# Gate products beside the row sums, transposes in TensorE's gaps, and vector work moved away from a norm and a search

## The chip, the cores and the metric

The kernel runs on one core of a Trainium2 chip. A core has five engines that work side by side, each through a queue of its own in order: TensorE (PE; its weight loads are listed as PEld), VectorE (DVE), ScalarE (ACT), GpSimd (POOL) and SyncE (SP, which issues most of the DMA transfers). They wait for each other by semaphores. The metric is the device time in microseconds (us); the time of a kernel is the median of its runs.

## The reference

Two transformer layers over 32 sequences ("batches") of 128 tokens, width 512, in float32. What matters here is the first layer, in which every step but the last is needed in full before the next can be closed:

```python
h = _ln(x, ln1_g, ln1_b) + shift
qkv = (h @ Wqkv.T).reshape(b, n, 3, H, HD)              # 16 heads of 64
q = _ln(q, qn_g, qn_b); k = _ln(k, kn_g, kn_b)          # per head
attn = softmax(q @ k.T / sqrt(HD)); o = attn @ v
x = x + o @ Wout.T
gate = softmax(tok @ Wgate.T)                            # 4096 tokens, 8 experts
vals, idx = top_k(gate.T, 512)                           # each expert takes 512 tokens
g = _ln(tok[idx], mlp_g, mlp_b)
y = gelu(g @ fc1s.T + b1s) @ fc2s.T + b2s                # per expert, hidden width 2048
tok = tok.at[idx].add(y * vals)
```

The second layer is attention (16 heads of 32) and an MLP, both with a scale and a shift that come from the condition vector ("adaLN").

## The kernel before

**Planner.** The kernel is not written in the order in which it runs. Each operation is registered with `sch.op(engine, us, fn, w=..., r=..., prio=..., job=...)`: its engine, an assumed duration, what it writes and reads, a priority (lower goes first) and a job. `Sched.run` then simulates the engines with these durations and emits for each engine, at every step, the operation that can start first, ties broken by the priority. A few jobs are open at once. Tiles come from four pools: 52 rows (`row`, 128 x 512 float32), small tiles (`sml`), the 8 PSUM banks (`bank`) and 11 weight slots. An operation whose tile has no free slot is not taken. `also=` names another engine that may do the operation: `tt` (L1130 on, its instructions at L1137 for VectorE and L1138 for GpSimd) uses it for elementwise sums, `copy` for copies by ScalarE or VectorE (L1128, L1129). Each engine executes its list in that fixed order.

**Start.** The projection of the condition (`ada`, L1197, into `pa`), the transposes of the first normed tokens (`tpx`), a small sum (`pu_a`), then the first qkv products (`pq`, L1316).

**Attention.** `pair(g)` takes two batches. All large products are done by a scheme of seven products of half size in place of eight, with sums of operands ahead (`os`, `tv`, `hsa`) and of results behind (`comb`, `onto`, `out2`). For each batch: the head norms by a Newton iteration on VectorE (`newton`, L299 to L307, whose result is `rs`), the scaling of q and k by it (L1463), transposes (`tpq`), scores (`sc`, L1495), exponentials (`pe`), row sums (`sums`, L1511, into `ps`) and the weighted values (`outs`, L1517). `back` does this for one batch, and the batch's gates.

**Gates.** The gate of a batch is linear in x and in the attention output, so it is computed from the transposed input (`xT`, loaded by `gate_T`) and `oT` without waiting for the projection: `gates` (L1553) puts twelve products of 32 columns into four strips of TensorE (`pgz`), the copy `zg` brings them to SBUF, and `add_up` (L1562) sums the strips by a product with a selection matrix (`pg`). A row-sum product uses TensorE in the same four strips. In a pair, the first batch's gates run in one operation with the second batch's row sums (`gates_sums`); the second batch's gates run by themselves. After each pair a softmax on VectorE and ScalarE writes `g_all` and a DMA adds the gates to the tokens' rows in `tok`.

**Late projections.** For the last 16 batches `oT` is stored (`otd`), and `late_projection` (through `project`, products `w` at L1595, additions to `xl`) runs during the choice of tokens.

**Choice of tokens** (from L1674). A search over 30 bits for each expert's 512th largest gate: count on VectorE (`junk`, L1691), sum over partitions on TensorE (`pc`, L1693), two updates on VectorE (`drop` L1695, `cand` L1697). Then prefix sums, and for each expert `expert_tokens(e)`: four one-hot tiles on VectorE (`oh`, L1762), values (`val`), 32 small products on TensorE (`pi`, L1782), and the indices `idx`.

**Experts.** `expert(e)` gathers its tokens by indirect DMA from GpSimd's queue (`xg`, L1826, which needs all stores to `tok`), norms them (`ng`), transposes them (`tpg`), and multiplies by `fc1` (`u`, L1935) and `fc2` (`d`, L1999). The sums of the `fc1` blocks (`s`, `fc`) are made by GpSimd, four for each of four blocks.

**Second layer.** At its beginning: `adaln` products (`pad`), the bias `pb0` (L2208), the norm of the first tokens and their transposes (`a_0t`), then the products `qk` (L2301).

Of the kernel before, what the change touches and what calls it, by code (L numbers as in the profile page):

```python
# [19 lines left out]
P = 128  # L20
# [225 lines left out]
def mm_us(n, count=1):  # L246

    return count * 2 * max(2 * n / 2400 + 0.0025, 0.11)
# [17 lines left out]
class Stage:  # L266
# [12 lines left out]
    def row(self, name, shape=(P, D)):  # L279
        return Buf(self.rows, list(shape), F32, name)  # L280

    def sml(self, name, n):
        return Buf(self.smls, [P, n], F32, name)
# [745 lines left out]
def fast_kernel(ctx: ExitStack, tc: tile.TileContext, x, condT, mask, cols, w_ada, wqkv, wout, wout_p, wout_o, wgate,  # L1029
# [17 lines left out]
    def const_tile(name, shape, dtype=F32):  # L1047
        return const.tile(list(shape), dtype, name=name)
# [6 lines left out]
    make_identity(nc, ident)  # L1055
    ones_f = const_tile("ones_f", (P, 64))
# [58 lines left out]
    def bcast(a, n):  # L1115

        return a.unsqueeze(2).to_broadcast([a.shape[0], a.shape[1], n])
# [32 lines left out]

    scratch, scratch2 = row("scratch", (P, D)), row("scratch2", (P, D))
# [136 lines left out]
    def pair(g):  # L1288
# [6 lines left out]
        lg, oT = sml(f"lg_{g}", 2 * E), []  # L1295
# [95 lines left out]
        for i in range(2):  # L1391
            sch.op(DVE, 0.19, lambda i=i: nc.vector.tensor_scalar(var[i].t, var[i].t, 1.0 / HD0, EPS, ALU.mult, ALU.add),
                   w=[var[i]], r=[var[i]], prio=pp + 10 + 100 * i, job=job)
            rs = st.newton(var[i], 2 * H0, f"qk_{b0 + i}", pp + 10 + 100 * i, job)
            if i == 0:
                zs, ahead = row(f"zg_{g}", (P, 2, S)), None
            oT_, ahead = back(b0 + i, i, job, lg, qk[i], v[i], rs, zs, ahead)
            oT.append(oT_)
        if b0 >= NB - LATE:
            late_projection(g)  # L1400
        else:
            project(g, oT, [x_b[b0], x_b[b0 + 1]], b0 * 100 + 142, job)

        pg = b0 * 100 + 150
        gm, gs = sml(f"gm_{g}", 2), sml(f"gs_{g}", 2)
        lv = lambda a: a.rearrange("p (n e) -> p n e", e=E)
        sch.op(DVE, 0.17, lambda: nc.vector.tensor_reduce(gm.t, lv(lg.t), AX.X, ALU.max), w=[gm], r=[lg], prio=pg, job=job)
        sch.op(DVE, 0.17, lambda: nc.vector.tensor_tensor(lv(lg.t), lv(lg.t), bcast(gm.t, E), ALU.subtract),
               w=[lg], r=[lg, gm], prio=pg, job=job)
        sch.op(ACT, 0.25, lambda: nc.scalar.activation(lg.t, lg.t, AF.Exp), w=[lg], r=[lg], prio=pg, job=job, table="exp")  # L1410
        sch.op(DVE, 0.17, lambda: nc.vector.tensor_reduce(gs.t, lv(lg.t), AX.X, ALU.add), w=[gs], r=[lg], prio=pg, job=job)
        sch.op(DVE, 0.17, lambda: nc.vector.reciprocal(gs.t, gs.t), w=[gs], r=[gs], prio=pg, job=job)
        sch.op(DVE, 0.17, lambda: nc.vector.tensor_tensor(
            g_all[:, b0 : b0 + 2, :], lv(lg.t), bcast(gs.t, E), ALU.mult), w=[(g_b, g)], r=[lg, gs], prio=pg, job=job)
        sch.op(SP, 0.06, lambda: nc.sync.dma_start(
            tok[b0 * S : (b0 + 2) * S, D:].rearrange("(b p) e -> p b e", p=P), g_all[:, b0 : b0 + 2, :]),
            w=[(tok_b, -1 - g)], r=[(g_b, g)], lat=3.0, prio=pg, job=job)

    statd = dram.tile([NB // 2, 4, S], F32, name="statd")
# [33 lines left out]
    def back(b, i, job, lg, qk, v, rs, zs, ahead):  # L1453
# [3 lines left out]
        late = b >= NB - LATE  # L1457
        qkT = [row(f"qkT_{b}_{j}", (P, 4, S)) for j in range(4)]
# [60 lines left out]
        if i == 0:  # L1519
            sch.op(PE, mm_us(D), sums, w=[ps], r=pe[0] + pe[1], prio=pa + 3, job=job)  # L1520
        else:

            def gates_sums(gates0=ahead[0]):
                gates0()
                sums()
            sch.op(PE, mm_us(S, 3) + mm_us(D), gates_sums, w=[ps, ahead[1]], r=pe[0] + pe[1] + ahead[2], prio=pa + 3, job=job)
            copy([(zs, 0)], [ahead[1]], lambda: zs.t[:, 0, :], lambda p_=ahead[1]: p_.t, S, pa + 3, job)
# [7 lines left out]
        def gate_T(pr):  # L1535

            t_ = row(f"xT_{b}", (P, DC, S))
            sch.op(SP, 0.06, lambda: nc.sync.dma_start(t_.t, xT[b]), w=[t_], r=[qkT[0]], lat=3.0, prio=pr, job=job)
            return t_
# [15 lines left out]
        if i:  # L1555
            pg = bank(f"pg_{b}", (P, 2, E))
            sch.op(PE, mm_us(S, len(parts) // DC), gates, w=[pz], r=need, prio=pgt, job=job)
            copy([(zs, 1)], [pz], lambda: zs.t[:, 1, :], lambda: pz.t, S, pgt, job)

            def add_up():  # L1560
                for n in range(2):
                    nc.tensor.matmul(pg.t[:, n, :], zs.t[:, n, :], sel[:, :E], start=True, stop=True)  # L1562
            sch.op(PE, mm_us(E, 2), add_up, w=[pg], r=[zs, cst_b], prio=pgt, job=job)
            sch.op(DVE, 0.16, lambda: nc.vector.tensor_copy(lg.t, flat(pg)), w=[lg], r=[pg], prio=pgt, job=job)
# [4 lines left out]
        return oT, (gates, pz, need)  # L1569
# [13 lines left out]
    def project(g, oT, xt, pr, job):  # L1583
        A = lambda i, j: oT[i - 1][j - 1]
        S_ = {i: row(f"os{i}_{g}", (P, 4, S)) for i in (1, 2, 3, 4)}
        for i, a_, b_, op_ in ((1, A(2, 1), A(2, 2), ALU.add), (2, S_[1], A(1, 1), ALU.subtract),
                               (3, A(1, 1), A(2, 1), ALU.subtract), (4, A(1, 2), S_[2], ALU.subtract)):
            tt(lambda i=i: S_[i].t, lambda a_=a_: a_.t, lambda b_=b_: b_.t, op_, D, [S_[i]], [a_, b_], pr - 1, job)
# [17 lines left out]
        def onto(a_, i, l):  # L1606

            tt(lambda: half(i, l), lambda: half(i, l), lambda: a_.t, ALU.add, HD, [(xt[i - 1], l)], [(xt[i - 1], l), a_], pr + 1, job)
# [45 lines left out]
    def late_projection(g):  # L1654
        pr = RP + 700 + 2 * g
        oT = [[row(f"ol_{2 * g + i}_{n}", (P, 4, S)) for n in range(2)] for i in range(2)]
        xt = [row(f"xl_{2 * g + i}") for i in range(2)]
        loads = [(oT[i][n], otd[2 * g + i - NB + LATE, n], [(otd_b, (2 * g + i, n))]) for i in (1, 0) for n in range(2)]
        for b_, src, r_ in loads + [(xt[i], x[2 * g + i], []) for i in range(2)]:
            sch.op(SP, 0.06, lambda b_=b_, src=src: nc.sync.dma_start(b_.t, src), w=[b_], r=r_, lat=3.0, prio=pr - 60, job=RJ, spare=20)  # L1660
        project(g, oT, xt, pr, RJ)
# [92 lines left out]

    def expert_tokens(e, pr, job, after=()):
# [28 lines left out]
        sch.op(PE, 1.0, gather, w=[pi], r=[*oh, val], prio=pr, job=job)  # L1784
        pv = lambda: pi.t.rearrange("p (h two) -> p h two", two=2)
# [25 lines left out]
    def expert(e, after):  # L1811
# [25 lines left out]
        for m in range(NM):  # L1837
# [11 lines left out]
            tt(lambda A=A, Sq=Sq: Sq(1), lambda A=A: A(2, 1), lambda A=A: A(2, 2), ALU.add, D, [(g, 1)], [(f, 1)], pw_, job, POOL, False)  # L1849
# [64 lines left out]
        if e == 0:  # L1914
            sums0.append(Tg[4])
            saw(PR + 5, job, [Tg[4]])
            expert_tokens(1, RP + 750, job)
# [287 lines left out]
    for i in (1, 2):  # L2205
        def bias0(i=i):
# [5 lines left out]
           prio=LB - 700, job=LJ)  # L2212

# [475 lines left out]
```

## Time and profile before

| | |
|---|---|
| median of 3 runs | 3215.75 us (3213.43 to 3215.94) |
| profiled execution, its time | 3212.72 us |
| its span, first to last instruction | 3211.0 us |
| TensorE busy | 3170.7 us |
| VectorE busy | 2262.4 us |
| ScalarE, GpSimd busy | 959.4, 713.1 us |
| mean granted TensorE clock | 0.996 |

The profile is one execution, recorded by the hardware profiler. Busy is the time in which an engine executes; the ends of matmuls are modelled, so that they overlap their successors by a little, and what counts is the distance from start to start. A line of the timeline gives start, duration, engine, source line, operation, `out<-in`, shapes, and `xN` for N merged instructions; in brackets stands the idle time before it. A wait names the engine that waited, what it was about to do, and what released it. PEclk is the share of TensorE's full clock that the chip granted. A float32 product shows as two matmul instructions.

By stages the execution goes: start to 14 us; attention to 965; late projections and choice of tokens to 1067; experts to 1877; second layer to the end.

### The profile page before, as it was taken

What the parts mean: (1) busy time and instruction counts of PE and PEld (TensorE: products, weight loads), DVE (VectorE), ACT (ScalarE), POOL (GpSimd) and SP (SyncE); (2) the same over time, 40 slices, a digit from 0 to 9 for tenths busy, and PEclk for the clock granted to TensorE, in tenths of its full rate; (3) what the DMA queues carried; (4) which work ended last, traced back from release to release, by engine and by line L of the source; (5) the groups of instructions that cost most, each with busy time, mean ns of one, the idle gap of its engine ahead of it and who ended that gap; (6) DMA issues with size and microseconds to landing.
All of it is one profiled execution on the core that took longest, in us unless ns stands there. A gap on an engine that the chain in (4) does not pass through costs nothing.

```text
span 3211.0 us, 55822 instructions
## 1 busy us (share of the span) xinstructions
PE 3170.7 (99%) x21688; PEld 2551.0 (79%) x21688; DVE 2262.4 (70%) x4895; ACT 959.4 (30%) x2299; POOL 713.1 (22%) x559
## 2 busy tenths in 40 slices
PE   8999999999999899999999999999999999999999
PEld 4655665555557788888888889999999999999998
DVE  8877777888867886766666447666666666666665
ACT  3333423444340222221122223333333333333332
POOL 0111111000034348776666500000000000000000
PEclk9999999999999899999999999999999999999999
DMA  4232223222235433344333553333333333333343
GB/s 175 73 103 70 73 71 115 100 99 70 66 121 186 141 92 115 102 112 119 96 110 88 167 184 112 96 98 100 101 101 103 106 105 101 100 101 100 99 138 107
DMA packets 253283, 346.44 MB, mean 108 GB/s; under 512 B 22810, under 2 KB 157522, under 8 KB 252498
## 3 DMA queue, kind: packets, MB, share of 16 engines
q1 hardware_dynamic: 244354, 325.16, 30.5%
q0 software_dynamic: 7168, 16.91, 2.8%
q8 instruction: 174, 2.85, 0.4%
q14 instruction: 99, 0.81, 0.1%
q10 hardware_dynamic: 1488, 0.71, 0.1%
HBM read 288.02 MB, written 54.69 MB: 107 GB/s over the span
## 4 chain that ended last, share of the span: by engine, by line
PE 96%; DVE 2%; DMA 1%; issue 0%; ACT 0%; POOL 0%; SPq 0%; ACTq 0%; DVEq 0%; POOLq 0%
PE m L2481 12%; PE n L2542 12%; PE u L1935 12%; PE d L1999 12%; PE q L1357 11%; PE qk L2301 6%; PE w L1595 6%; PE v L1357 5%; PE v L2347 3%; PE o L2347 3%; PE sc L1495 2%; PE po L1517 2%; PE tpq L1113 2%; PE pq L1316 1%; PE sc L2397 1%; PE ps L1511 1%
## 5 line engine op out<-in xcount | busy, mean ns | idle before, releaser
L2428 POOL TENSOR_TENSOR hi_t<-hi_t,inv 128x512 f32<-128x512 f32 x32 | 40.7, 1272 | 1218.6 <-DVE inv L1148 1218.6
L2492 ACT ACTIVATE m<-m,prm 128x128 f32<-128x128 f32 x512 | 161.8, 389 | 236.6 <-DVE m L2486 232.1
L1999 PE MATMUL d<-fc,h 128*128 128x256 f32 x992 | 219.0, 380 | 0.0
L1999 PEld LDWEIGHTS d<-fc,h 128*128 128x128 f32 x992 | 188.4, 190 | 24.9
L1946 ACT ACTIVATE h<-h,prm 128x256 f32<-128x256 f32 x256 | 115.0, 500 | 256.8 <-DVE h L1940 256.8
L1935 PE MATMUL u<-gT,fc 128*128 128x256 f32 x768 | 179.6, 384 | 0.7 <-ACT gT L1902 0.7
L1935 PEld LDWEIGHTS u<-gT,fc 128*128 128x128 f32 x768 | 148.1, 193 | 21.5 <-ACT gT L1902 1.1
L2486 DVE TENSOR_TENSOR m<-mu,m 128x512 f32<-128x512 f32 x128 | 87.9, 688 | 104.4 <-PE m L2481 101.8
L1323 ACT ACTIVATE sq<-qk 128x512 f32<-128x512 f32 x128 | 81.4, 636 | 220.4 <-DVE qk L1361 212.0
L2486 DVE TENSOR_TENSOR mu<-mu,m 128x512 f32<-128x512 f32 x96 | 65.9, 686 | 85.3 <-PE m L2481 85.1
L2481 PE MATMUL m<-n2a,w_s 128*128 128x128 f32 x1024 | 125.0, 276 | 0.0
L1940 DVE TENSOR_TENSOR h<-v,u 128x512 f32<-128x512 f32 x128 | 86.6, 683 | 50.8 <-PE u L1935 49.1
L2542 PE MATMUL n<-w_t,ms 128*128 128x256 f32 x512 | 122.3, 383 | 0.0
L1935 PE MATMUL u<-tg,s 128*128 128x256 f32 x512 | 121.1, 380 | 0.8 <-DVE tg L1137 0.8
L2481 PE MATMUL m<-n2T,w 128*128 128x128 f32 x1024 | 119.9, 276 | 0.0
L2481 PEld LDWEIGHTS m<-n2a,w_s 128*128 128x128 f32 x1024 | 119.6, 192 | 0.1
L2481 PEld LDWEIGHTS m<-n2T,w 128*128 128x128 f32 x1024 | 118.2, 192 | 1.2 <-DVE n2T L2236 0.2
L2542 PE MATMUL n<-w_t,m 128*128 128x256 f32 x512 | 116.3, 380 | 0.0
L2542 PE MATMUL n<-w,m 128*128 128x256 f32 x512 | 114.7, 383 | 0.0
L1357 PE MATMUL q<-wqkv,hT 128*128 128x512 f32 x240 | 114.5, 605 | 0.0
L1999 PE MATMUL d<-t,hs 128*128 128x256 f32 x512 | 113.5, 380 | 0.0
L1357 PE MATMUL q<-wqkv,hsb 128*128 128x512 f32 x240 | 113.4, 595 | 0.0
(1225 smaller groups left out, 7486.5 us busy)
## 6 DMA issues: line engine op xcount, KB each, us to landing
w_t<-t2d SPq DMA_DIRECT2D x256, 256.0 KB, 3.1
w<-in_w_dram SPq DMA_DIRECT2D x192, 256.0 KB, 4.4
fc<-in_fc_dram SPq DMA_DIRECT2D x64, 512.0 KB, 4.5
fc<-in_fc_dram SPq DMA_DIRECT2D x32, 1024.0 KB, 5.3
x<-in_x_dram SPq DMA_DIRECT2D x32, 256.0 KB, 3.0
xT<-in_xT_dram SPq DMA_DIRECT2D x32, 256.0 KB, 2.7
otd<-oT SPq DMA_DIRECT2D x32, 256.0 KB, 2.1
ol<-otd SPq DMA_DIRECT2D x32, 256.0 KB, 4.3
```

The lines of the kernel that those rows point to most:

```text
L1357: nc.tensor.matmul(ps[m].t, lhs()[:, k, :], rhs[0](k), start=(k == 0), stop=(k == 1))
L1595: nc.tensor.matmul(ps[n].t, lhs.t[:, k, :], rhs(k), start=(k == 0), stop=(k == 3))
L1935: nc.tensor.matmul(ps[n].t[:, t, :], lhs()[:, k, t * P : (t + 1) * P], rhs.t[:, k, :], start=(k == 0), stop=(k == 1))
L1940: sch.op(DVE, dve_us(D), lambda: nc.vector.tensor_tensor(o_.t, a_.t, ps[n].t, ALU.add), w=[o_], r=[a_, ps[n]], prio=pr, job=job)
L1946: sch.op(ACT, act_us(HQ, 1), lambda t=t, c=c: nc.scalar.activation(o_.t[:, t, :], o_.t[:, t, :], AF.Gelu_apprx_tanh, bias=col("b1s", e * 1 ...
L1999: nc.tensor.matmul(ps[n].t[:, j, :], lhs[m].t[:, k, t * P : (t + 1) * P], rhs.t[:, 2 * m + k, :], start=(m == 0 and k == 0), stop=(m == NM ...
L2301: nc.tensor.matmul(ps[m].t[:, z, u, :], w_()[:, k, u * P : (u + 1) * P], rhs()[:, k, :], start=(k == 0), stop=(k == 1))
L2347: nc.tensor.matmul(ps[m].t, lhs()[:, k, :], w_()[:, k, :], start=(k == 0), stop=(k == 1))
L2481: nc.tensor.matmul(ps[n].t[:, u, :], l1w[what].t[:, k, (NQ * q + u) * P : (NQ * q + u + 1) * P], rhs()[:, k, :], start=(k == 0), stop=(k = ...
L2486: sch.op(DVE, dve_us(D), lambda: nc.vector.tensor_tensor(o_.t, a_.t, ps[n].t, ALU.add), w=[o_, *more], r=[a_, ps[n]], prio=pq_, job=job)
L2492: sch.op(ACT, act_us(S, 1), lambda u=u, c=c: nc.scalar.activation(o_.t[:, u, :], o_.t[:, u, :], AF.Gelu, bias=col("b1", c), scale=1.0), w= ...
L2542: nc.tensor.matmul(ps[n].t, Ah[lhs][c // NQ].t[:, c % NQ, :], b_.t[:, k, :], start=(c == 0), stop=(c == 7))
```

## The change

- **Gates.** Every batch's gate products but the last batch's now run with the next batch's row sums, over the border of the pair too (`gq["ahead"]`). `close` copies the strips of four batches into one tile and, at the fourth, sums them (`pg`, read by the softmax straight from PSUM), does one softmax for four batches and one store. The load of `xT` is issued after the second half of `oT` instead of after `qkT`, but for the last batch.
- **Transposes.** `spin(n, dst)` transposes the identity matrix n times into a bank that nobody reads: 44 at the very start, 62 after the last late projection (`ends["xt"]`), 28 after the small products of expert 1's indices (`pis[1]`), 22 after the bias product `pb0` of the second layer.
- **GpSimd.** The first of the four sums of each `fc1` block of expert 0 now also waits for the head norm of the last batch (`ends["rs"]`). In the late projections the sums and additions may no longer go to GpSimd (`also=False`).
- **One-hots.** Those of expert 1 now wait for the last late projection.

```diff
+    def spin(n, dst):
+        for _ in range(n):
+            nc.tensor.transpose(dst[:, :P], ident, ident)
...
+    spun = bank("spun")
+    sch.op(PE, 6.5, lambda: spin(44, spun.t), w=[spun], prio=-2000, job=0)
...
-            if i == 0:
-                zs, ahead = row(f"zg_{g}", (P, 2, S)), None
-            oT_, ahead = back(b0 + i, i, job, lg, qk[i], v[i], rs, zs, ahead)
-            oT.append(oT_)
+            oT.append(back(b0 + i, i, job, qk[i], v[i], rs))
...
+    def close(b, pz, pr, job):
+
+        if b % 4 == 0:
+            gq["zs"] = row(f"zg_{b}", (P, 4, S))
+        zs, n = gq["zs"], b % 4
+        copy([(zs, n)], [pz], lambda: zs.t[:, n, :], lambda: pz.t, S, pr, job)
+        if n < 3:
+            return
+        q, b0 = b // 4, b - 3
+        pg, lg, gm, gs = bank(f"pg_{q}", (P, 4, E)), sml(f"lg_{q}", 4 * E), sml(f"gm_{q}", 4), sml(f"gs_{q}", 4)
+
+        def add_up():
+            for k in range(4):
+                nc.tensor.matmul(pg.t[:, k, :], zs.t[:, k, :], sel[:, :E], start=True, stop=True)
+        sch.op(PE, mm_us(E, 4), add_up, w=[pg], r=[zs, cst_b], prio=pr + 2, job=job)
...
+        sch.op(DVE, 0.19, lambda: nc.vector.tensor_reduce(gm.t, pg.t, AX.X, ALU.max), w=[gm], r=[pg], prio=pr, job=job)
...
+        if b == NB - 1:
+            ends["rs"] = rs
...
-        if i == 0:
+        if b == 0:
             sch.op(PE, mm_us(D), sums, w=[ps], r=pe[0] + pe[1], prio=pa + 3, job=job)
         else:
 
-            def gates_sums(gates0=ahead[0]):
+            gates0, pz0, need0 = gq["ahead"]
+
+            def gates_sums():
                 gates0()
                 sums()
...
+            sch.op(PE, mm_us(S, 3) + mm_us(D), gates_sums, w=[ps, pz0], r=pe[0] + pe[1] + need0, prio=pa + 3, job=job)
+            close(b - 1, pz0, pa + 3, job)
...
-            sch.op(SP, 0.06, lambda: nc.sync.dma_start(t_.t, xT[b]), w=[t_], r=[qkT[0]], lat=3.0, prio=pr, job=job)
+            sch.op(SP, 0.06, lambda: nc.sync.dma_start(t_.t, xT[b]), w=[t_], r=[qkT[0] if b == NB - 1 else oT[1]], lat=3.0,
+                   prio=pr, job=job)
...
-        if i:
-            pg = bank(f"pg_{b}", (P, 2, E))
+        gq["ahead"] = (gates, pz, need)
+        if b == NB - 1:
             sch.op(PE, mm_us(S, len(parts) // DC), gates, w=[pz], r=need, prio=pgt, job=job)
...
+            close(b, pz, pgt, job)
...
+        ends["xt"] = xt
...
-        project(g, oT, xt, pr, RJ)
+
+        project(g, oT, xt, pr, RJ, also=False)
...
-            tt(lambda A=A, Sq=Sq: Sq(1), lambda A=A: A(2, 1), lambda A=A: A(2, 2), ALU.add, D, [(g, 1)], [(f, 1)], pw_, job, POOL, False)
+            tt(lambda A=A, Sq=Sq: Sq(1), lambda A=A: A(2, 1), lambda A=A: A(2, 2), ALU.add, D, [(g, 1)], [(f, 1), *([] if e else [ends["rs"]])], pw_, job, POOL, False)
...
-            expert_tokens(1, RP + 750, job)
+
+            expert_tokens(1, RP + 750, job, ends["xt"])
+            spun0, spun2 = bank("spun0"), bank("spun2")
+            sch.op(PE, 6.7, lambda: spin(62, spun0.t), w=[spun0], r=ends["xt"], prio=RP + 740, job=job)
+            sch.op(PE, 3.0, lambda: spin(28, spun2.t), w=[spun2], r=[pis[1]], prio=RP + 990, job=job)
...
+    spun1 = bank("spun1")
+    sch.op(PE, 2.4, lambda: spin(22, spun1.t), w=[spun1], r=[pb0], prio=LB - 820.5, job=LJ)
```

## The prediction

> **What bounds it now.** I read the page first: busy times, clock row, chain of waits.
>
> ```profile
> span 3211.0 us, 55822 instructions
> ...
> PE 3170.7 (99%) x21688; PEld 2551.0 (79%) x21688; DVE 2262.4 (70%) x4895; ACT 959.4 (30%) x2299; POOL 713.1 (22%) x559
> ...
> PEclk9999999999999899999999999999999999999999
> ...
> PE 96%; DVE 2%; DMA 1%; issue 0%; ACT 0%; POOL 0%; SPq 0%; ACTq 0%; DVEq 0%; POOLq 0%
> ```
>
> TensorE sets the end. Time is saved only by fewer TensorE cycles, less TensorE idling, or a clock that doesn't drop. Second, the waits of TensorE (total, times, longest): they are the whole list of its idling worth more than 1.5 us.
>
> ```profile
> PE tpg L1113 <- DVE xng L1890: 10.2, 1, 10.2
> PE pa L1197 <- DMA wada<-in_w_ada_dram: 8.4, 1, 8.4
> PE tpq L1113 <- DVE qk L1463: 3.1, 1, 3.1
> PE a_0t L1113 <- DVE a_1v L339: 2.8, 1, 2.8
> PE pc L1693 <- DVE junk L1691: 2.1, 4, 0.8
> PE sc L1495 <- DVE qkT L1475: 1.8, 2, 1.6
> ```
>
> Third, the clock. The trace grants half clock in 66.6-70.0, 1070.1-1087.2 and 1889.3-1896.1 us and, by the spacing of the matmuls, before 12.0. I asked for busy times by stretch on the clock's own grid (length, then PE, PEld, DVE, ACT, POOL, clock):
>
> ```profile
> 8.57:11.98 3.41, 3.41 (x16) 1.75 (x15) 1.56 (x6) 0.59 (x1) 0.00 (x0) 1.00 1.05 399
> 937.00:940.40 3.40, 1.58 (x10) 1.32 (x11) 3.37 (x6) 0.78 (x1) 3.22 (x3) 1.00 0.19 69
> 1080.35:1083.77 3.42, 2.76 (x7) 2.20 (x8) 2.53 (x9) 2.01 (x6) 0.85 (x1) 0.50 0.92 323
> 1885.90:1889.31 3.41, 1.09 (x6) 0.61 (x4) 2.35 (x9) 1.07 (x4) 0.00 (x0) 1.00 1.05 407
> ```
>
> A full stretch (first) is followed by full clock; one 81% busy (third) isn't. One with 1.09 us of matmuls (last) is followed by half clock, while the second, 1.58 us busy of which about 1.0 are transposes, keeps full clock. So transposes seem to count as activity. Fourth, the timeline around two gate products (start, duration):
>
> ```profile
> 700.35 0.43 PE L1553 MATMUL pgz<-xT,wg 128*32 128x128 f32 x8
> 700.59 0.62 PE L1553 MATMUL pgz<-oT,ww 128*32 128x128 f32 x16
> 701.02 1.04 PE L1511 MATMUL ps<-pe,ones_f 128*32 128x512 f32 x8
> 701.88 1.93 PE L1517 MATMUL po<-pe,v 128*32 128x128 f32 x64
> ...
> 705.57 1.88 PE L1357 MATMUL q<-wqkv,hsb 128*128 128x512 f32 x4
> 707.38 0.43 PE L1553 MATMUL pgz<-xT,wg 128*32 128x128 f32 x8
> 707.62 0.62 PE L1553 MATMUL pgz<-oT,ww 128*32 128x128 f32 x16
> 708.17 1.98 PE L1357 MATMUL q<-wqkv,hT 128*128 128x512 f32 x4
> ```
>
> And VectorE beside a GpSimd sum and without one:
>
> ```profile
> 931.33 1.26 POOL L1138 TENSOR_TENSOR s<-fc 128x512 f32<-128x512 f32 x1
> 931.44 1.20 DVE L303 SCALAR_TENSOR_TENSOR qk_31t<-qk_31y 128x32 f32<-128x32 f32 x1
> ...
> 935.04 0.19 DVE L303 SCALAR_TENSOR_TENSOR qk_30t<-qk_30y 128x32 f32<-128x32 f32 x1
> ```
>
> **What the Trainium skill says.** "TensorE: Matmul & The Clock Gate", Part 1: the clock is half after an idle window of about 3.4 us and full after a busy one, the window running freely; the grid above agrees. Its Part 4 says full clock doesn't engage for transposes; the second stretch speaks against that, but no run here has transposes alone. "TensorEngine Tiling (Array Packing)", Key Properties: changing the tiling mode drains TensorE; the trace agrees, about 0.1 us each way (below). "SBUF — State Buffer", SBUF: two separate sides: a VectorE instruction with two SBUF inputs and a GpSimd one that reads SBUF exclude each other for a whole instruction; the 1.20 against 0.19 us agrees.
>
> **The change, step by step**, against the profiled execution (3212.72 us; span 3211.0 and 1.7 around it). The median of the runs, 3215.75, lies 3.0 above it; I carry the difference over to the median.
>
> *Gates beside row sums.* A gate product alone: the four q products ahead take 1.81 (705.57 to 707.38) where 4 x 0.43 = 1.72 is their rate, so 0.1 goes to the switch; then 0.79 to the next product. Beside row sums it takes 0.67 (700.35 to 701.02), the switch is already paid by the sums, and these take 0.86 instead of 0.88 where they follow a q product. Saved: 0.10 + 0.12 + 0.02 = 0.24, in the 15 pairs that have a successor: 3.6. The adding up (0.36 and 0.1 of switch per pair, 16 times: 7.4) becomes 8 times 0.72 + 0.1: 6.6, saves 0.8. Together **-4.4** (ends -3 and -5). The small VectorE and ScalarE instructions and the stores of the gates halve, the copy of the sums goes; VectorE is 70 to 84% busy in that stage under a TensorE without idling, so this counts nothing. The load of xT waits for oT instead of qkT: behind it on SP's queue stand the loads of the next pair; it takes 2.7 us to land and is needed only at the next batch's row sums (13 or some 40 us later), so nothing. Without that cover it would be a wait of 2.7 per batch. Three rows of the pool (xT, two oT) are held some 40 us longer in each pair: the profile shows no rows; nothing if there is slack, bounded above under the rivals.
>
> *44 transposes at the start.* Transposes start 0.213 us apart at half clock, 0.107 at full. From 1.6 us (the identity is ready at 1.53), 3.4 to 6.8 us at half clock and the rest at full: end at 8.0 to 9.7, against the weight's landing at 8.43. Then pa takes 1.04 (the row of ps, same shape) instead of 1.94, and eight transposes 1.04 instead of 1.89; the first q product, at 13.83 now, comes 0.5 to 1.3 earlier: **-1.0**. If they stay at half clock, they end at 11.0: +2.6.
>
> *GpSimd's first-expert sums wait for the last norms.* Now three of batch 31's Newton steps take 1.20 to 1.30 instead of 0.19 beside them, ahead of batch 30's on VectorE's queue: these start at 934.8, though their squares are there at 929.7, and TensorE waits 3.1 and then 1.6 us. With the sums behind both norms I give all but a rest back: **-4.2** (0 to -4.7). The 16 sums of 1.27 then run from about 935 to 956; their products stand at 1081, so they have 120 us.
>
> *Late projections on VectorE alone.* In 979-1041 VectorE is busy 50.4 of 62 us; 15 of the 30 updates of the candidate take 0.77 instead of 0.16 beside GpSimd: 9 us go. GpSimd's 24 instructions there come over: 12 x 0.69 + 12 x 0.42 = 13.3. So 54 of 62, and the 2.1 us of waits at pc partly go: **-1.0** (-2 to +8, see the rivals).
>
> *One-hots of expert 1 into the gap, 62 and 28 transposes.* The four one-hots (1.22 each) now delay VectorE's last additions at 1060-1067; without them and GpSimd's additions the last store starts some 0.3 earlier, and so do the gathers. VectorE then does the one-hots from 1067.5 to 1072.5, before the first gathered row lands (1074.6). TensorE: 62 x 0.107 = 6.6 from 1067.5, the product of the indices 0.9, 28 x 0.107 = 3.0: to 1078.0, against 1077.9 for the first transposes. At full clock these end 0.5 earlier, the sixteen products at 1081.01 take 3.5 instead of 6.75; the next transposes then wait for VectorE's xng, which follows the evictions, some 0.5: **-3.9**. Bounds: -4.6 without that wait; +6.4 if the transposes run at half clock after one window: 32 x 0.107 + 30 x 0.213 = 9.8, 0.9, 28 x 0.213 = 6.0, end at 1084.3.
>
> *22 transposes at 1887.* 2.4 us in a gap of 2.8, no delay. Products at half clock in 1889.3-1896.1 cost up to 3.4, but the one at 1897.6 needs VectorE's sums n1a, ready at 1895.5: **-2.0** (-3.4 to +1).
>
> Sum: -4.4 - 1.0 - 4.2 - 1.0 - 3.9 - 2.0 = -16.5: 3196.2 for the profiled execution, **3199.3 us** for the median.
>
> **Rivals.** (1) *Transposes don't hold the clock* (Part 4 of that page): +2.6, +6.4 and +1.0 at the three places, and -9.6 of the rest: +0.4, 3216. Against it: the stretches at 8.57 and 937. (2) *VectorE becomes the bound of the choice of tokens*, the slower side: with its own steps and the projections' additions on one engine, each of the 30 rounds waits for one addition of 0.69: +20.7, and the -1.0 goes: -15.5 + 20.7 = +5.2, 3221; from 0.73 us a round on it is slower than before by more than 0.2%. For it: 54 of 62 us; against it: a round needs about 1.4 us of a product's 1.83, and half of them bear 0.6 of GpSimd now. (3) *Half the gain is lost to the new order*: the planner orders everything anew, and the rows held longer may move loads; a stall of 0.5 us in each of 15 pairs gives back 8: 3207. (4) *The gaps only move*: the clock and norm waits recur elsewhere; only the gates' 4.4 remains: 3211.
>
> **How the numbers follow.** Forecast 0.70 (its own range 3192 to 3206), rival 3 0.13, rival 4 0.05, rival 1 0.06, rival 2 0.06. 0.2% (6.4 us, to 3209.3) is about what a measurement tells from no change. Faster: all of the forecast, most of rival 3: 0.81; same: rivals 1, 4, the rest of 3, half of 2: 0.13; slower: 0.06. The range from 3190 (every part at its better end gives -21.0, 3194.8; the 3.0 between median and profiled execution may be half-clock windows that the change takes away too) to 3211 holds the forecast, rival 3 and part of 4.
>
> **What would show it.** Right: no half clock at 1070-1087 and 1889-1896; tpg's wait gone from the list; no wait of tpq on qk around 935; gate products always followed by ps except the last; junk's waits under 2 us. Wrong: transposes 0.213 apart in the gap; pc waiting for junk many times; new waits of PE in 100-900 us.

## The result, and the profile after

The changed kernel takes 3198.31 us (median of 5, 3196.16 to 3199.16), the kernel before, measured beside it, 3213.43 (median of 5, 3211.29 to 3215.94). The ratio is 0.9951, its 95% interval 0.9940 to 0.9963: the change saves about 0.5%. The profiled execution took 3197.88 us, of which the span is 3196.2.

The page of the changed kernel, the lines that answer to the first ones shown of before:

```profile
span 3196.2 us, 56046 instructions
...
PE 3178.3 (99%) x21844; PEld 2564.6 (80%) x21844; DVE 2255.1 (71%) x4867; ACT 961.9 (30%) x2306; POOL 668.7 (21%) x516
...
PEclk9999999999999999999999999999999999999999
...
PE 97%; DVE 2%; DMA 0%; issue 0%; ACT 0%; POOL 0%; SPq 0%; DVEq 0%; ACTq 0%; POOLq 0%
```

TensorE is still the bound. It executes 156 products more than before, all of them the added transposes, and yet ends 14.8 us earlier: what went was idling and half clock. The clock row has lost its 8.

TensorE's waits in the changed kernel (total, times, longest):

```profile
PE spun L1060 <- POOL ident masks.py:199: 1.6, 1, 1.6
PE q L1364 <- DVE hT L1465: 1.5, 1, 1.5
PE tpx L1118 <- DVE xn L1450: 1.3, 1, 1.3
PE pgz L1578 <- DVE oT L1556: 1.2, 2, 1.0
PE tpq L1118 <- DVE qk L1485: 1.0, 1, 1.0
...
PE u L1963 <- DVE tg L1142: 0.8, 1, 0.8
PE tpg L1118 <- DVE xng L1914: 0.8, 2, 0.6
```

The waits of 10.2, 8.4, 3.1 and 2.8 us are gone, and so is the wait of `pc` on `junk`. Three lines are new beside those of the transposes: `q` on `hT` (at 100.7 us), the wait of `tpq` on `qk` at 133 us, and `pgz` on `oT` (the longer one at 965 us).

Where the time went is best read from places that both kernels pass. The table gives what each stretch takes more (+) or less (-) than in the kernel before, by the trace, for this kernel and for those of the next section; b4 is the start of the row sums of batch 4, and so on.

| stretch | after | gates only (e1) | no gates (e2) | no transposes (e3) | GpSimd helps (e4) | sums free (e5) | one-hots back (e6) | statistics later (e7) | two mends (e8) | the changed kernel again (e9) | mended, no gates (e10) | mends and fill (e11) |
|---|---|---|---|---|---|---|---|---|---|---|---|---|
| start to b0 | -0.80 | +0.47 | +0.42 | +2.58 | -0.50 | -0.83 | +1.05 | -0.39 | -2.50 | -2.33 | -2.19 | -2.53 |
| b0 to b4 | +1.91 | +1.92 | -0.01 | +1.94 | +1.94 | +1.93 | +1.93 | +1.91 | +0.19 | +1.92 | +0.33 | +0.19 |
| b4 to b28 | -3.04 | -3.04 | 0.00 | -3.05 | -3.04 | -3.04 | -3.05 | -4.80 | -4.81 | -3.05 | 0.00 | -4.81 |
| b28 to b31 | -4.99 | -0.34 | -5.17 | -4.98 | -4.98 | +1.33 | -4.99 | -4.98 | -4.98 | -4.98 | -5.17 | -4.98 |
| b31 to the last output product | -2.32 | -0.50 | -3.71 | -2.33 | -0.49 | -3.94 | -2.32 | -2.34 | -2.33 | -2.31 | -3.72 | -2.32 |
| to the 17th `u` product | -3.44 | -0.88 | -3.23 | -1.12 | -3.25 | -3.47 | -3.74 | -1.95 | -1.44 | -2.27 | -2.40 | -2.27 |
| to the end | -2.15 | -0.21 | -1.88 | -0.05 | -1.98 | -2.12 | -1.95 | -1.73 | -1.08 | -1.98 | -2.03 | -1.81 |
| span against before | -14.83 | -2.58 | -13.58 | -7.01 | -12.30 | -10.14 | -13.07 | -14.28 | -16.95 | -15.00 | -15.18 | -18.53 |

The rows in the middle repeat to 0.03 us from kernel to kernel wherever the order of the work is the same. The first row and the last two don't: e9 is the changed kernel once more, and differs from it by 1.5, 1.2 and 0.2 us there. These rows hold the stretches in which the clock may fall, which the last section comes back to, and also the gathers and the last store. From the last output product to the first `tpg` the changed kernel takes 11.2 us in one execution and 12.4 in the other (e9); in e8 the span ends 0.8 us later after the last product than in e9. So a difference of 1 or 1.5 us in these rows says nothing about an edit by itself.

### The profile page after: what moved, and what is told of

It is laid out like the page before. It is cut to its first block, busy times and chain, and to the rows that moved or that the text cites. A ratio compares the mean times of both kernels' runs of the same rounds, so it can differ in the third digit from the quotient of the medians.

```text
span 3196.2 us, 56046 instructions
## 1 busy us (share of the span) xinstructions
PE 3178.3 (99%) x21844; PEld 2564.6 (80%) x21844; DVE 2255.1 (71%) x4867; ACT 961.9 (30%) x2306; POOL 668.7 (21%) x516
## 4 chain that ended last, share of the span: by engine, by line
PE 97%; DVE 2%; DMA 0%; issue 0%; ACT 0%; POOL 0%; SPq 0%; DVEq 0%; ACTq 0%; POOLq 0%
PE m L2511 13%; PE n L2572 12%; PE d L2027 12%; PE u L1963 12%; PE q L1364 11%; PE qk L2331 6%; PE w L1615 6%; PE v L1364 5%; PE v L2377 3%; PE o L2377 3%; PE sc L1517 2%; PE po L1539 2%; PE tpq L1118 2%; PE pq L1323 1%; PE sc L2427 1%; PE ps L2438 1%
## 5 line engine op out<-in xcount | busy, mean ns | idle before, releaser
L1364 PE MATMUL q<-t,hsa 128*128 128x512 f32 x240 | 112.8, 592 | 0.0
```

What stands on the lines that cost most here:

```text
L1364: nc.tensor.matmul(ps[m].t, lhs()[:, k, :], rhs[0](k), start=(k == 0), stop=(k == 1))
```

## The experiments

All were timed in five rounds against the kernel before; e1 has 13 runs, e3 has 9, the others 5.

| run | median, us (lowest to highest) | ratio (95%) | span of the profiled execution |
|---|---|---|---|
| e1, gates alone | 3211.63 (3209.49 to 3215.51) | 0.9997 (0.9989 to 1.0005) | 3208.4 |
| e2, all but the gates | 3199.22 (3198.00 to 3201.68) | 0.9956 (0.9943 to 0.9970) | 3197.4 |
| e3, all but the transposes | 3205.88 (3203.64 to 3208.14) | 0.9976 (0.9966 to 0.9986) | 3204.0 |
| e4, late additions on GpSimd too | 3200.11 (3199.70 to 3201.05) | 0.9957 (0.9943 to 0.9970) | 3198.7 |
| e5, GpSimd's sums free | 3202.38 (3201.53 to 3202.67) | 0.9962 (0.9948 to 0.9975) | 3200.8 |
| e6, one-hots back | 3197.68 (3196.75 to 3199.64) | 0.9948 (0.9934 to 0.9961) | 3197.9 |
| e7, statistics later | 3195.03 (3194.46 to 3198.43) | 0.9940 (0.9926 to 0.9954) | 3196.7 |
| e8, two mends | 3194.84 (3193.30 to 3195.77) | 0.9937 (0.9924 to 0.9951) | 3194.0 |
| e9, the changed kernel again | 3198.93 (3197.72 to 3200.81) | 0.9956 (0.9942 to 0.9970) | 3196.0 |
| e10, mended, no gates | 3197.85 (3197.53 to 3200.58) | 0.9954 (0.9940 to 0.9968) | 3195.8 |
| e11, mends and fill | 3194.37 (3194.11 to 3194.92) | 0.9942 (0.9928 to 0.9955) | 3192.5 |

e1 to e4, e5 to e8 and e9 to e11 ran together. The kernel before varies by some 2 us from group to group (medians of 3212.0, 3214.6 and 3213.2 us), so within a group the medians say more than the ratios. The changed kernel's 3198.31 us stands in none of the three: a difference of 1 or 2 us from it is read from the trace, by stretches, and not from the medians.

### e1: the gates part alone

The changed kernel with every other part taken out:

```diff
-    sch.op(PE, 6.5, lambda: spin(44, spun.t), w=[spun], prio=-2000, job=0)
-        project(g, oT, xt, pr, RJ, also=False)
+        project(g, oT, xt, pr, RJ)
-... [(f, 1), *([] if e else [ends["rs"]])], pw_, job, POOL, False)
+... [(f, 1)], pw_, job, POOL, False)
-            expert_tokens(1, RP + 750, job, ends["xt"])
-            sch.op(PE, 6.7, lambda: spin(62, spun0.t), ...)
-            sch.op(PE, 3.0, lambda: spin(28, spun2.t), ...)
+            expert_tokens(1, RP + 750, job)
-    sch.op(PE, 2.4, lambda: spin(22, spun1.t), ...)
```

> The kernel before with the gates' part alone (no transposes, GpSimd and one-hots as before). Theory: the gate products save 0.58 us per two pairs, as worked out, but the planner's new order gives most of it back: waits of TensorE between 95 and 140 us (+1.8 by the row sums of batch 4) and the small transposes of the norms (pst) put between two halves of the scores (+0.58 per two pairs up to batch 16). So about -1.3 us against before, and both marks in the profile. Rival: the waits at 95 to 140 us come from the 44 transposes at the start, which shift the plan; then they are absent here and the gain is about 3 us.

Measured: the ratio can't be told from 1, and the span fell by 2.6 us. The trace divides this: 3.0 gained from b4 to b28, 1.9 lost before b4, and some small gains late. The loss before b4 is there without the 44 transposes, so the rival, by which these cause it, is ruled out. The last norms and the two long gaps stay as they were. TensorE's longest waits in this run:

```profile
PE tpg L1118 <- DVE xng L1912: 9.7, 1, 9.7
PE pa L1202 <- DMA wada<-in_w_ada_dram: 8.6, 1, 8.6
PE sc L1515 <- DVE qkT L1495: 3.2, 2, 3.0
PE a_0t L1118 <- DVE a_1v L339: 2.9, 1, 2.9
```

So the gates do not touch the big waits, and they don't bring by themselves what was expected of them.

### e2: everything but the gates

`back`, `pair` and the order of the gates as before; all else as in the changed kernel:

```diff
-            oT.append(back(b0 + i, i, job, qk[i], v[i], rs))
+            if i == 0:
+                zs, ahead = row(f"zg_{g}", (P, 2, S)), None
+            oT_, ahead = back(b0 + i, i, job, lg, qk[i], v[i], rs, zs, ahead)
+            oT.append(oT_)
-    def close(b, pz, pr, job):
...
```

> The changed kernel without the gates' part. Theory: the same two marks are absent, the row sums of batch 4 start no later against the first q product than before, and the time is 13.5 us under before (1.3 above the changed kernel). Rival (the 44 transposes shift the plan): TensorE still waits about 2.7 us between 95 and 140 us, and the time is some 11 us under before.

Measured: 0.9 us above the changed kernel in the median. By the trace, the two are equal from b0 on: -14.00 against -14.03 us to the end, and -8.89 against -8.44 in the four rows that repeat. The loss before b4 is absent and so is the gain after it; the stretch from b31 to the last output product is 1.4 us shorter than in the changed kernel. In the presence of the other parts the gates are worth nothing, for three reasons that can be seen.

The first is at 100 us. The timeline of TensorE in the changed kernel (start, duration):

```profile
97.58 1.89 PE L1615 MATMUL w<-wout,os 128*128 128x256 f32 x8
100.02 0.27 PE L1309 MATMUL pst<-ident,n_2mv 128*4 128x128 f32 x1 [0.55 <-DVE n_2mv L1308]
100.12 0.60 PE L1118 MATMUL tpx<-ident,xn 128*128 128x128 f32 x4
102.22 1.55 PE L1364 MATMUL q<-t,hT 128*128 128x512 f32 x3 [1.49 <-DVE hT L1465]
```

and in e2:

```profile
98.16 0.60 PE L1118 MATMUL tpx<-ident,xn 128*128 128x128 f32 x4
98.60 1.88 PE L1364 MATMUL v<-wqkv,hT 128*128 128x512 f32 x4
100.32 1.92 PE L1364 MATMUL q<-t,hT 128*128 128x512 f32 x4
```

In the changed kernel the planner has used up the `v` products earlier, in place of the gate products that are no longer there, and has put the next pair's statistics (`pst`) ahead of this pair's transposes (`tpx`). `xn` was ready at 91.5 us, but `tpx` stands behind `pst`, and nothing is left to cover the copy to `hT`. With 1.02 us of a wait at 133 us, these new waits come to 3.1 us, where the kernel before waits 0.35.

The second lies in the pairs from b4 to b16, and e7 takes it up. The third is at 965 us: the last batch's gates have no row sums to follow, and wait 1.03 us for `oT`; behind them eight products of `pg` in a row take 0.81 us where four took 0.36.

### e3: everything but the transposes

```diff
-    sch.op(PE, 6.5, lambda: spin(44, spun.t), w=[spun], prio=-2000, job=0)
-            sch.op(PE, 6.7, lambda: spin(62, spun0.t), ...)
-            sch.op(PE, 3.0, lambda: spin(28, spun2.t), ...)
-    sch.op(PE, 2.4, lambda: spin(22, spun1.t), ...)
```

> The changed kernel without the four groups of transposes. Theory: they hold the clock, and they are worth 0.65 (start) + 3.6 (gap ahead of the experts) + 2.0 (start of the second layer) = 6.2 us; half clock returns for some 17 us after the gap and up to 7 us at the second layer, the first q product comes 0.65 later. Rival: what the gap gives comes from the earlier stores and gathers, and the transposes give it nothing: then 2.7 us, with the first tpg to the ninth as far apart as in the changed kernel (6.2 us).

Measured: 7.6 us slower than the changed kernel in the median, 7.8 in the span. The four groups are taken out together here, and only the place in the trace tells them apart. The 7.8 lie in three stretches: 3.4 before b0, 2.3 in the gap, 2.1 in the second layer. The 3.4 are more than the transposes are worth there, since in this execution the full clock came only at 17.9 us (12.0 in the kernel before). TensorE's waits between 1050 and 1080 us in e3:

```profile
PE tpg L1118 <- DVE xng L1913: 5.2, 1, 5.2
PE pi L1804 <- DVE oh L1784: 4.0, 4, 1.7
```

With the one-hots in the gap and no transposes, 9.2 us of it are idle; half clock runs from 1065.8 to 1079.5 us. The changed kernel, in the same stretch:

```profile
1057.57 6.93 PE L1060 MATMUL spun<-ident 128*128 128x128 f32 x62
1064.34 0.95 PE L1805 MATMUL pi<-val,oh 128*128 128x8 bf16 x32
1065.15 3.26 PE L1060 MATMUL spun<-ident 128*128 128x128 f32 x28
1068.58 0.66 PE L1118 MATMUL tpg<-ident,xng 128*128 128x128 f32 x4 [0.17 <-DVE xng L1914]
...
1071.07 3.72 PE L1963 MATMUL u<-gT,fc 128*128 128x256 f32 x16 [0.59 <-ACT gT L1926]
```

62 transposes take 6.77 us from the first to the `pi` behind them, 0.109 each: full clock through more than six microseconds in which TensorE did nothing else. The sixteen `u` products take 3.7 us; before they took 6.6. From the first `tpg` to the 17th `u` it is 10.53 us before, 9.70 in e3 and 7.22 in the changed kernel, in both of its executions. Counted from the first `tpg`, this leaves out when the first gathered row lands.

### e4: late additions on GpSimd as well

```diff
-        project(g, oT, xt, pr, RJ, also=False)
+        project(g, oT, xt, pr, RJ)
```

> The changed kernel with the late projections' sums and additions allowed on GpSimd again. Theory: GpSimd's reads block the search's updates (0.77 instead of 0.16 us each), TensorE waits at pc again for about 2 us, the 30 rounds take 59 us instead of 55, and the kernel is 2.3 us slower than the changed one. Rival: TensorE's products set the pace of the search in both, the gain came with the earlier norms of the last pair: 0 to 0.5 us.

Measured: 1.8 us slower than the changed kernel in the median. In the trace the stretch from b31 to the last output product is 1.84 us longer. Busy times from 979 to 1041 us (length, then PE, PEld, DVE, ACT, POOL, clock), in the changed kernel:

```profile
979.00:1041.00 62.00, 62.00 (x306) 52.20 (x306) 56.49 (x201) 1.86 (x5) 0.00 (x0) 1.00 0.52 176
```

and in e4, with its wait:

```profile
979.00:1041.00 62.00, 61.92 (x301) 50.93 (x300) 49.11 (x176) 1.86 (x5) 21.82 (x24) 1.00 0.51 175
```

```profile
PE pc L1714 <- DVE junk L1712: 0.6, 1, 0.6
```

VectorE has 7.4 us more to do in the changed kernel and is 91% busy, and TensorE still never waits for it: the 30 rounds take 55.0 us from the first `pc` to the last, against 57.0 in e4 (59 had been expected) and 59.4 in the kernel before. Taking GpSimd away shortens what it was slowing: the update `cand` takes 0.16 us in all 30 rounds of the changed kernel, while in e4 ten of the 30 take 0.23 to 1.04.

### e5: GpSimd's sums free again

```diff
-... [(f, 1), *([] if e else [ends["rs"]])], pw_, job, POOL, False)
+... [(f, 1)], pw_, job, POOL, False)
```

> The changed kernel, but GpSimd's sums for the first expert no longer wait for the last Newton steps. Theory: these sums run beside the last norms again and stretch VectorE's small steps to about 1.2 us; the stretch from the row sums of batch 28 to those of batch 31 then grows by about 5 us (the changed kernel gained 5.0 us there), while the pairs before stay: 3203 us, ratio to the kernel before 0.997. Rival: the 5.0 us came from the new order of the gates and the projections; then the stretch grows by less than 1 us and the time is 3198 to 3199.

Measured: 3202.4 us; the span rises by 4.7. From b28 to b31 it takes 6.3 us more than the changed kernel, and then 1.6 less to the last output product, since the last gates no longer wait. VectorE's steps of batch 31's norm in the changed kernel:

```profile
933.41 0.19 DVE L303 SCALAR_TENSOR_TENSOR qk_31t<-qk_31y 128x32 f32<-128x32 f32 x1
933.64 0.19 DVE L305 TENSOR_TENSOR qk_31t<-qk_31t,var 128x32 f32<-128x32 f32 x1
933.86 0.19 DVE L307 SCALAR_TENSOR_TENSOR qk_31y<-qk_31t,qk_31y 128x32 f32<-128x32 f32 x1
```

and in e5, first VectorE's, then what GpSimd does beside them:

```profile
935.91 1.19 DVE L303 SCALAR_TENSOR_TENSOR qk_31t<-qk_31y 128x32 f32<-128x32 f32 x1
937.14 1.31 DVE L305 TENSOR_TENSOR qk_31t<-qk_31t,var 128x32 f32<-128x32 f32 x1
938.48 1.19 DVE L307 SCALAR_TENSOR_TENSOR qk_31y<-qk_31t,qk_31y 128x32 f32<-128x32 f32 x1
```

```profile
935.79 1.26 POOL L1143 TENSOR_TENSOR s<-fc 128x512 f32<-128x512 f32 x1
937.13 1.27 POOL L1143 TENSOR_TENSOR s<-s,fc 128x512 f32<-128x512 f32 x1
938.35 1.27 POOL L1143 TENSOR_TENSOR fc<-fc 128x512 f32<-128x512 f32 x1
```

Each small step ends with a GpSimd addition: 0.19 becomes 1.2. This agrees with what the Trainium skill's "SBUF — State Buffer" (section "SBUF: two separate sides") says of the port pair that the two engines share: one of them holds it for a whole instruction. With the wait undone, nothing of the gain of the stretch is left, so the rival, the new order, did not bring it; that e5 takes 1.3 us more there than even the kernel before is not followed up.

### e6: the one-hots back among the last additions

```diff
-            expert_tokens(1, RP + 750, job, ends["xt"])
+            expert_tokens(1, RP + 750, job)
```

> The changed kernel with the second expert's one-hots back among the last additions, the 62 and 28 transposes kept. Theory: the one-hots delay the last additions by at most 0.3 us, and the gap's gain is the clock that the transposes hold; the distance from the last output product to the first transpose of gathered rows stays at 11.2 to 11.4 us and the time rises by 0.2 to 0.6 us: 3198.5 to 3199. Rival: moving the one-hots is itself worth about what the last additions wait for them, four of 1.22 us less what is hidden: the time rises by 2 us or more, to 3200 or above.

Measured: 3197.68 us, and no run reaches the rival's 3200. From b0 to the end the two differ by 0.1 us, and the distance from the last output product to the first `tpg` is 10.91 us here, 11.22 there; the 12.38 of e9 show that 0.3 is less than one kernel varies by. No gain from moving the one-hots can be seen. That the transposes make the gap's gain is shown by e3.

### e7: the statistics transposed later

```diff
-... nc.tensor.transpose(pst.t, mv.t, ident), w=[pst], r=[mv], prio=prn - 400, job=job)
+... nc.tensor.transpose(pst.t, mv.t, ident), w=[pst], r=[mv], prio=prn - 240, job=job)
```

> The changed kernel with the transpose of the row statistics given a later due time, so that it stands beside the products again and not between the two halves of the scores. Theory: the gates gain nothing in the pairs from batch 4 to 18 because this transpose costs 0.18 us more and the scores 0.40 us more there; with it moved, each two pairs take 0.58 us less, some 2 us over the stretch, and the opening waits at 99 to 103 us stay: 3196.3 us, ratio 0.9945. Rival: in these pairs the rhythm is set by another engine; the sum over two pairs stays at 127.8 us and the time at 3198.

Measured: 3195.03 us, below both the theory and the rival. In the kernel before none of the 14 transposes of statistics stands between scores; in the changed kernel, and in e1 and e3, six do. The timeline of the changed kernel:

```profile
383.40 1.16 PE L1517 MATMUL sc<-qkT,qkT 64*128 64x128 f32 x16
384.49 0.27 PE L1309 MATMUL pst<-ident,n_7mv 128*4 128x128 f32 x1
384.69 1.16 PE L1517 MATMUL sc<-qkT,qkT 64*128 64x128 f32 x16
```

and of e7, whose 32 scores run through:

```profile
383.22 2.06 PE L1517 MATMUL sc<-qkT,qkT 64*128 64x128 f32 x32
385.21 1.98 PE L1364 MATMUL v<-tv,hT 128*128 128x512 f32 x4
...
388.75 0.27 PE L1309 MATMUL pst<-ident,n_7mv 128*4 128x128 f32 x1
```

From 383.40 to 385.78 the changed kernel takes 2.38 us for the scores and `pst`; e7 takes 1.99 for the scores and 0.11 for `pst`. The scores use 64 of TensorE's rows at a time, `pst` all 128: between the scores it brings two more changes of tiling mode. The 0.28 us are measured; that these changes are their cause is read from the shapes. The time from b8 to b12 is 127.777 us before, 127.785 after and 127.202 in e7. So the gates did gain their 0.58 in these two pairs, and `pst` gave it back. Over b4 to b28 the trace shows 1.76 us; the medians differ by 3.3 across groups and by 2.65 against e6 in its own group.

### e8: two mends

```diff
+        if j:
+            spun3 = bank("spun3")
+            sch.op(PE, 1.2, lambda: spin(11, spun3.t), w=[spun3], r=[pu], prio=130, job=1)
-... w=[pst], r=[mv], prio=prn - 400, job=job)
+... w=[pst], r=[mv], prio=prn - (100 if g == 2 else 240), job=job)
```

> The changed kernel with that later due time, the first statistics transpose behind the transposes of the second pair, and 11 more transposes of the identity after the second product of the gates' weights, in the wait of 1.3 us at 64.6 us. Theory: the half clock at 65.6 to 69.0 us goes (worth some 1.2 us), and the opening waits fall by 0.5 to 1 us, on top of the 2 us of the other run: 3194 to 3195 us. Rival: the softmax of batch 0 on ScalarE sets the first row sums whatever the clock, and the opening waits only move: 3196, as in the other run.

Measured: 3194.84 us, in the range expected. At 100 us `tpx` now stands ahead of `pst`; one wait of 1.36 us for `hT` is left of the three, and the row sums of b4 come 2.3 us earlier than before (1.1 later in the changed kernel). But the median is only 0.2 below e7's. In the profiled execution of e8 the clock fell at 1066.8 us, and the stretch from the last output product to the 17th `u` takes 0.8 us more than in e11, 2.0 more than in the changed kernel. e7's profiled execution lost the clock there too, and was the slowest of its five. How often that happens the medians don't tell; that the mended opening is worth the 3.8 us by which b4 comes earlier than in e7 isn't shown by the times. Only 1.7 of the 3.8 lie behind b0, where the order is mended. The rest goes with the half clock near 65 us: the three kernels with the eleven transposes don't have it, nine of the ten executions without them do, and in the tenth (e9) the row sums of batch 0 come only 0.2 us after e8's.

### e9, e10, e11: the gates again, in a mended order

e9 is the changed kernel as it is. e10 is e2 with the eleven transposes at 64 us. e11 is e8 with five transposes behind each of the first two `tpg`:

```diff
             sch.op(PE, 4 * TR, lambda tp=tp, xn=xn: transpose4(tp.t, xn.t), w=[tp], r=[xn], prio=px[h], job=job)
+            if e == 0 and h < 2:
+                fill = bank(f"fill_{h}")
+                sch.op(PE, 0.5, lambda fill=fill: spin(5, fill.t), w=[fill], r=[tp], prio=px[h], job=job)
```

> The changed kernel once more, as the measure for the two runs beside it: 3198 us, ratio 0.995.

> The changed kernel without its gates part, with the 11 more transposes of the identity at 64.6 us. Here the statistics transposes stand beside the products anyway. Theory: once the order is mended the gates part is worth what a pair shows without disturbance, 0.58 us per two pairs or some 4 us of the 14 pairs, less 1 to 1.5 us at the choice of tokens; so this kernel is 2.5 to 3.5 us slower than the one with both mends: 3197 to 3198 us, and the sums of batches 8 to 12 lie 127.78 us apart against 127.20. Rival: the gates part is worth nothing net even then, and this kernel takes 3194 to 3195 us.

> The kernel with the two mends, and five more transposes of the identity behind each of the first two sets of transposes of gathered rows. Theory: they fill the waits of 0.77 and 0.52 us, no window of half clock comes at 1066.8 to 1070.2 us, and the sixteen products after them take 3.7 us, not 5.5: 3192 to 3193 us, ratio 0.993. Rival: that window came by the phase in which the clock's windows fell and goes in some executions anyway; the fill delays the next transposes by some 0.1 us each and the time stays at 3194 to 3195 us.

Measured on one chip: 3198.93, 3197.85 and 3194.37 us. e11 and e10 differ by the gates (and the fill), 3.5 us in the median and 3.3 in the span, and their runs do not overlap. The trace puts -4.8 from b4 to b28 and +1.4 from b31 to the last output product between them, and from b8 to b12 it has the 127.78 us of e10 against 127.20 that were expected. The fill is no part of this: to the 17th `u` e11 gains 0.1 us less than e10. The gates part is thus worth some 3.4 us where its surroundings are put right, and nothing where they aren't.

The gap in e11:

```profile
1064.52 0.66 PE L1118 MATMUL tpg<-ident,xng 128*128 128x128 f32 x4 [1.15 <-DVE ng_1t L322]
1065.01 0.71 PE L1060 MATMUL fill<-ident 128*128 128x128 f32 x5
1065.77 0.66 PE L1118 MATMUL tpg<-ident,xng 128*128 128x128 f32 x4
1066.27 0.71 PE L1060 MATMUL fill<-ident 128*128 128x128 f32 x5
1067.01 3.72 PE L1969 MATMUL u<-gT,fc 128*128 128x256 f32 x16
```

The waits are filled and the sixteen products run at full clock, 3.8 us to the next `tpg` against 5.3 in e8, but the first `tpg`, ahead of any fill, starts 0.55 us later than there, and `u` with it. That is not the fill's doing: e9 and e10, beside e11 and without a fill, are as late (12.38 and 12.28 us after the last output product, 12.37 in e11, 10.9 to 11.8 in all other traces). Nor have e9 and e10 half clock there, so the expectation's rival, chance, stands. The median, 0.5 below e8's and in another group, came out where the rival had it; whether the fill brings anything stays open. That e11 beats the changed kernel is plain: it is 4.6 us (0.14%) below it in the same group, and no run of the one reaches those of the other.

## Why the prediction was right, and where it was not

The forecast was 3199.3 us; the result is 3198.3. That it is so close is in part luck. Two errors offset each other: the sum of the steps was 16.5 for the profiled execution, which fell by 14.8, and the 3.0 us by which the median had stood above the profiled execution were carried over, where the changed kernel shows 0.4. Most of that is the median of the kernel before itself, 3213.43 when measured beside the changed one and 3215.75 earlier. The steps themselves offset each other too. By the trace, with e2 for the share of the gates, the start gave -0.8, GpSimd's sums -5.2, the stretch from b31 to the last output product -3.7, the gap -3.4 and the second layer -2.1 us, and the gates +0.4.

**Gates, -4.4: the step that failed.** The gain of two undisturbed pairs is 0.58 us (b20 to b24: 103.61 to 103.03), and the step gives the same: 2 x 0.24 + (2 x 0.46 - 0.82). Its terms were off both ways: the row sums, gate products and what stands beside them fell by 0.84, not 0.48, and the adding up rose by 0.26 (eight `pg` in a row take 0.99, four take 0.36) where a fall of 0.10 was given. What failed is the assumption that the pairs stay as they are but for this. It is the mechanism of rival 3, the planner's new order, at a smaller size and in the gates alone: +2.7 of waits at 99 to 134 us, `pst` between the scores (0.58 per two pairs from b4 to b16, 1.8 in all), and +1.4 at the last batch, where `pgz` waits for `oT`. Against this stands one gain that wasn't foreseen: a wait of 1.2 us for the statistics at 630 us went with the old order. Net: +1.92 before b4, -3.04 to b28, +0.18 to b31 and +1.39 to the last output product, which is 0.45 us lost where 4.4 were to be saved (e2).

**44 transposes, -1.0.** The first `q` product of the start came 0.65 earlier, the row sums of batch 0 0.80 (in e9, without half clock at 65 us, 0.91 and 2.33). The transposes ended at 9.45 us, inside the 8.0 to 9.7 given, but `hT` is waited for 0.8 us as before.

**GpSimd's sums behind the norms, -4.2.** Confirmed by e5. It measured -4.99 in the stretch, but the gates' own gain is no part of that (e2 has -5.17 without them). That is 0.8 to 1.0 more than given, and more than the waits of 3.1 and 1.6 us that were to go: they went wholly, though the step had left a rest, and where the remaining 0.3 to 0.5 lay was not followed up.

**Late additions on VectorE, -1.0.** -1.8 (e4). The sign that rival 2 rested on, VectorE's busy share, came out at 56.5 of 62 us, above the 54 worked out, and no round waited. The step's term was right: each round needs less of VectorE than a product's time. The stretch gained more than e4 gives back. Its 407 output products take 95.4 us from start to start before, and 91.1 in the changed kernel and in every other run without GpSimd there; with it they take 94.5 in e1 and 92.9 in e4. So what GpSimd costs depends on where its instructions fall among the search's updates, and 2.5 of the 4.3 us are no sure part of this edit; the list of waits had shown 2.1. (Of the 30 updates 14 were long, not 15, with 0.82 us in the mean; the sum of 9 us is the same.)

**The gap, -3.9.** -3.4 to the 17th `u` product, of which 3.3 lie behind the first `tpg`, where the clock no longer falls; in e9 it is -2.3, since the first `tpg` comes later. Without the transposes 2.3 of the 3.4 go (e3); the 1.1 that stay there are one stretch of half clock fewer than before and an earlier `tpg`. The terms that the step names make -3.55 (0.3 + 0.5 + 3.25 - 0.5), so neither its -3.9 nor its bound of -4.6 follows from them. Measured, the first `tpg` is 0.1 earlier where 0.3 was given (and e6 shows nothing from the one-hots), from there to the first `u` it takes 0.6 less where 0.5 was given, and the sixteen products take 2.9 less where 3.25 was given. The wait of the next `tpg` that was subtracted did not appear.

**22 transposes at 1887, -2.0.** -2.15, and -0.05 without them (e3).

Rival 1 is ruled out: the transposes hold the clock. Rival 4 also: the waits of these gaps did not come back elsewhere. "New waits of PE in 100-900 us" was named as a sign of error; they were there, 3.1 us before b4 and so most of what the gates were to save.

## What to carry to other kernels

Where a planner orders the work, a saving must be looked for between two marks on either side of it, not in the total: here a saving of 0.58 us per two pairs was made and spent again, by one small transpose that moved between products of another tiling mode. An operation that keeps TensorE awake is cheap only inside a wait, and there it is worth the products at half clock that follow. When two engines share a port, the longer instruction sets the pace of the shorter ones: move the long ones behind the chain, or onto the other engine, even when that is then 91% busy as VectorE was here.

## What was not expected of the hardware

**Transposes alone hold and raise the clock.** The Trainium skill, "TensorE: Matmul & The Clock Gate", Part 4, says that full clock doesn't engage for them. For the float32 transposes of this kernel it did: it came at 7.6 us, after nothing but transposes of the identity from 1.6 us on, whose spacing fell from 0.213 to 0.109 us there, and it stayed through 62 of them at 1057.6 to 1064.3.

**No single busy share decides the next window.** In each of the thirteen traces the changes of the clock lie within 0.03 us of a grid of 3.4133 us: in the kernel before they come at 66.59, 70.01, 1070.12 and 1087.18, which are 1, 293 and 5 steps apart. Two stretches of the grid and what follows them (length, PE, PEld, DVE, ACT, POOL, clock), in e4:

```profile
1069.98:1073.39 3.41, 1.91 (x14) 1.19 (x12) 2.57 (x11) 1.87 (x6) 2.50 (x4) 1.00 0.75 181
1073.39:1076.80 3.41, 3.38 (x16) 2.95 (x16) 2.75 (x11) 1.85 (x5) 0.76 (x1) 1.00 0.97 313
```

and in e7:

```profile
1066.63:1070.05 3.42, 1.97 (x13) 1.25 (x12) 2.66 (x9) 2.15 (x6) 2.50 (x4) 1.00 0.69 183
1070.05:1073.46 3.41, 3.41 (x9) 2.70 (x9) 2.75 (x11) 1.14 (x5) 0.53 (x1) 0.50 1.03 353
```

1.91 us of TensorE keep the full clock, 1.97 lose it; and the 1.58 us at 937 us in the kernel before keep it. At the four places where it falls in some kernel (62, 937, 1070 and 1885 us), stretches at full clock with 0.9 to 1.8 us of idling were followed by either; with more than 1.9 by half clock only, with less than 0.9 by full. To come back took more: stretches at half clock were followed by half again with 0.52 and 0.65 us of idling (before, at 1889.3 and 1080.4 us) and by full with 0.31 and 0.47 (the changed kernel at 65.6, e3 at 14.5). Busy times have modelled ends, and what else counts stays open.

**The grid's place varies from execution to execution.** The changed kernel has half clock from 65.6 to 69.0 us in one profiled execution and none in another (e9), where full clock first came at 7.59 and at 6.84 us; this puts the row sums of batch 0 1.5 us apart; e2 and e6 have it for two stretches. Whether a gap of 1 to 2 us costs the clock is therefore partly a matter of chance, and two spans that differ by less than 2 us must be compared mark by mark.
